# A decoder layer on one core: division order, statistics order, first feed-forward quarters and the output bias

## The chip, the core and the metric

The kernel runs on one NeuronCore of a Trainium2 chip. The profile names its engines PE (TensorE, matrix products and transposes), DVE (VectorE), ACT (ScalarE), POOL (GpSimd) and SP (SyncE, which issues most transfers). PE writes only to PSUM, from where DVE and ACT take results; POOL works in SBUF. The metric is the device time of one execution in microseconds (us), as the median of several runs.

## The reference

A pre-norm decoder layer on x of 8 batches x 256 rows x 1024 features, all in float32:

```python
x = x + attn(layernorm(x))            # 32 heads of 32, binary weights with scales
x = x + xattn(layernorm(x), ctx)      # 16 heads over a context of 256 rows, low-rank keys and values
x = x + ffn(layernorm(x))

# ffn, INTER = 2752, RANK = 256
P = x @ U1
H = P @ V1 + b1
act = silu(H[..., :INTER]) * H[..., INTER:]
out = (act @ U2) @ V2 + b2
```

In the attentions the scores of a head go through a softmax: subtract the row's maximum, take the exponential, divide by the row's sum. In the cross-attention the context is projected once to 64 features (`C_kv = K @ Wkv_d`), which serve as keys and, projected up, as values.

## The kernel before

The work is tiled by 128 rows. One batch of 256 rows is two tiles. There are three phases, one after the other: self-attention of batches 0 to 7, cross-attention of batches 0 to 7, and the feed-forward in four blocks of four tiles (512 rows).

**Steps.** Both attentions run as a chain of steps: eight per batch in self-attention, four in cross-attention, four heads each. `step` (L676) issues the scores of its heads, the row maxima on DVE (L686, `nm`), the transposes of the step before's probabilities (`turned`, L518, copied by ACT at L526), the exponentials on ACT (L705, `p`), and at its end the weighted sums of the step before. What a step before the last still owes (`early` and `late`, for example the rescaled cross-attention output `y` at L667, which POOL adds to x at L674) stands in between.

**Parts.** Between these a step runs *parts*: pieces of other work that keep PE busy, such as projections of the next batch. A plan written out by hand (`self_plan`, `cross_plan`) says which parts go into which step, and the order of instructions on each engine is exactly the order in which the program issues them. `run_part` (L192) takes one part off the queue. A part may have a preparation of its own (`ahead`) that is issued before its main work; up to two parts marked `soon` have theirs issued at the start of the step (L691).

**Divisions.** In self-attention the probabilities are divided by their sums: a reciprocal (L556), then four multiplications by DVE (L566), or POOL or ACT for some heads. `step` issues the divisions of a pair of heads just before a part, as soon as the exponentials of that pair have been issued (the inner function `then`).

**Context parts.** In self-attention step 5 of the last batch, the parts are four transposes of the first cross-attention context (`ctx_parts`, L783, PE L163), copied in turn by ACT and DVE (L789, `cT`), and the projection that reads them (`ckv_part`, L799). In the other batches' context parts the step is a cross-attention step.

**Statistics.** The means and variances for the layer norms are pieces of DVE work (L138, L140, `statistics`), kept in the list `idle`. `run_part` issues one ahead of a part when enough credit has built up, which the parts' estimated lengths add to. A reader that needs them earlier takes all that are left (`need`). After a tile's last piece POOL computes the inverse deviation (L121, L122). In cross-attention the finished x of a batch leaves to memory from POOL's queue (`x_leave`, L872) in step 2 of the next batch.

**First feed-forward quarters.** `head_parts` (L975) normalizes a half of a tile (DVE L155, `xn`, two buffers), transposes it on PE (L997) and copies it out, by ACT or DVE in turn (L998, `xT`). A block has eight of these, and then two factors (L1008). Those of block 0 are the parts of the last cross-attention batch, four in each of steps 0 and 1; those of the later blocks run beside the block before. Their PSUM tile comes from the pool `psA` with two banks. Most other parts call `bank` (L107), which goes round three banks, two of `psA` and one of `psB`.

**Feed-forward.** For each of 22 column tiles of 128 (the last of 64), `hidden` makes gate and up (PE L1034), ACT the sigmoid (L1046), DVE the products (L1047, L1049), and `down` sums them two iterations later (PE L1078). `tail` (L1093) multiplies by V2 (PE L1097), adds b2 on DVE into `y` (L1105), adds `y` to x on POOL (L1107) and stores a tile of 512 KB (L1108). The tails of a block run in iterations 2 to 5 of the next block; those of the last block end the kernel.

Of the kernel before, what the change touches and what calls it, by code (L numbers as in the profile page):

```python
# [10 lines left out]
F32 = mybir.dt.float32  # L11
# [7 lines left out]
P = 128  # L19
# [16 lines left out]
def decoder_layer(  # L36
# [24 lines left out]
    nc = tc.nc  # L61
    B, S, E = x.shape
    NT = B * S // P
    TB = S // P
# [42 lines left out]
    def bank(shape, name):  # L107
        turn[0] += 1
        if turn[0] % 3 == 1:
            return psB.tile(shape, F32, tag="psB", name=name)  # L110
        return psA.tile(shape, F32, tag="psA", name=name)
# [38 lines left out]
    mv3 = [stat.tile([P, TB, 2], F32, name=f"mv3_{b}") for b in range(B)]  # L150
    rs3 = [stat.tile([P, TB], F32, name=f"rs3_{b}") for b in range(B)]

    def normed_half(x_, mv, rs, h):
        xn = wk_.tile([P, 512], F32, tag="xn", name="xn", bufs=2)
        nc.vector.tensor_scalar(  # L155
            xn, x_[:, h * 512 : (h + 1) * 512], mv, rs, ALU.subtract, ALU.mult
        )
        return xn
# [13 lines left out]
    def settle():  # L172
        now = list(ripe)
        ripe[:] = later
        later.clear()
        for f in now:
            f()
# [1 line left out]


    class Part:
        def __init__(self, us, main, ahead=None, soon=False):
            self.us, self.main, self.todo, self.soon = us, main, ahead, soon

        def ahead(self):
            if self.todo is not None:
# [2 lines left out]

    queue = []  # L190

    def run_part(then=None):  # L192

        settle()
        if idle and credit[0] > 2.0:
            credit[0] -= 2.0
            idle.pop(0)()
        if then is not None:
            then()
        p = queue.pop(0)  # L200
        p.ahead()
        if queue:
            queue[0].ahead()
        p.main()
        credit[0] = min(credit[0] + p.us, 4.5) if idle else 0.0


    qT_w = [wt.tile([P, EC, P], F32R, tag=f"qw{c}", name=f"qT_w{c}") for c in range(EC)]
# [467 lines left out]
    def step(cur, prev, parts, extra=None):  # L676

        s = cur.scores()
        nm = small.tile([P, 4, TB], F32, tag="nm", name="nm")
        cur.sm = small.tile([P, TB, 4], F32, tag="sm", name="sm")  # L680
        due = prev.prev if prev is not None else None
        if due is not None:
            due.early()
        pTs = []
        for j in range(4):
            nc.vector.tensor_reduce(nm[:, j, :], s[j], AX.X, ALU.max, negate=True)  # L686
            if prev is not None:
                pTs.append(turned(prev.p[j]))
        for p in queue[: min(parts, 2)]:
            p.ahead()  # L690
        soon = [p for p in queue[:parts] if p.soon][:2]  # L691
        if isinstance(due, Cross):
            for p in soon:
                p.ahead()
        if due is not None:
            due.late()
        for p in soon:
            p.ahead()
        cur.p, cur.prev = [], prev
        exps = []  # L700

        def exp(j, t):
            if t == 0:
                cur.p.append(wk_.tile([P, TB, S], F32, tag="p", name="p", bufs=4))
            nc.scalar.activation(  # L705
                cur.p[j][:, t, :], s[j][:, t, :], AF.Exp,
                bias=nm[:, j, t : t + 1], accum_out=cur.sm[:, t, j : j + 1],
            )

        exps = [(j, t) for j in range(4) for t in range(TB)]  # L710


        divided = isinstance(cur, Self)
        pe, sc = 0.0, (0.5 if prev is not None else 3.0) if divided else 1.0
        pairs = [0, 1]
        for k in range(parts):
            pe += queue[0].us
            while exps and sc < pe:
                exp(*exps.pop(0))
                sc += 0.49  # L720

            if divided and not pairs and queue[0].us > 1.0:
                cur.over_sums_end()

            def then():
                while k and divided and pairs and len(exps) <= 4 - 4 * pairs[0]:
                    cur.over_sums(pairs.pop(0))

            run_part(then)
            if k == 0 and extra is not None:  # L730
                extra()
        for e in exps:
            exp(*e)
        for i in pairs:
            cur.over_sums(i)
        cur.over_sums_end()
        if not parts and extra is not None:
            extra()
        if prev is not None:
            prev.weighted(pTs)  # L740
            prev.prev = None
        return cur
# [40 lines left out]
    def ctx_parts(st, copies):  # L783
        def main(q):
            t, h = q // 2, q % 2
            if q == 0:
                st.cT = wk_.tile([P, EC, S], F32, tag="xh", name="cT")
            ps = four_T(st.c[t][:, h * 512 : (h + 1) * 512], "ps_c")
            copies[h](st.cT[:, h * 4 : (h + 1) * 4, t * P : (t + 1) * P], ps)  # L789

        return [Part(0.5, lambda q=q: main(q)) for q in range(2 * TB)]

    def ckv_part(st):
        def main():
# [180 lines left out]
    def head_parts(fb):  # L975


        def ahead(q):
            j, h = q // 2, q % 2
            b = fb.i * 2 + j // TB  # L980
            need(fb.half[j // TB])
            fb.xn = getattr(fb, "xn", {})
            fb.xn[q] = normed_half(
                fb.x[j], mv3[b][:, j % TB, 0:1], rs3[b][:, j % TB : j % TB + 1], h
            )

        def main(q):
            j, h = q // 2, q % 2
            if q == 0:
                fb.xT = [  # L990
                    wk_.tile([P, 4, W], F32, tag="qT", name="xT0", bufs=2),
                    wk_.tile([P, 4, W], F32, tag="xl", name="xT1"),
                ]
            ps = psA.tile([P, 4, P], F32, tag="psA", name="ps_t")
            xn = fb.xn.pop(q)
            for k in range(4):
                nc.tensor.transpose(ps[:, k, :], xn[:, k * P : (k + 1) * P], ident)  # L997
            (dve if h else act)(fb.xT[h][:, :, j * P : (j + 1) * P], ps)  # L998

        def factor(r):  # L1000
            if r == 0:
                if fb.i % 2 == 0:
                    fb.pT = wk_.tile([P, RC, W], F32, tag="xh", name="pT")
                else:
                    fb.pT = fw.late[:, 0:RC, :]
            ps = psA.tile([P, W], F32, tag="psA", name="ps_p")
            for e in range(EC):
                nc.tensor.matmul(  # L1008
                    ps,
                    fw.u1[:, e, r * P : (r + 1) * P],  # L1010
                    fb.xT[e // 4][:, e % 4, :],
                    start=(e == 0),
                    stop=(e == EC - 1),
                )
            (dve if r else act)(fb.pT[:, r, :], ps)

        return [Part(0.5, lambda q=q: main(q), lambda q=q: ahead(q), True) for q in range(2 * BT)] + [
            Part(7.0, lambda r=r: factor(r)) for r in range(RC)
        ]
# [73 lines left out]
    def tail(fb, j):  # L1093
        for h in range(E // 512):
            ps = psA.tile([P, 512], F32, tag="psA", name="ps_o")
            for r in range(RC):
                nc.tensor.matmul(  # L1097
                    ps,
                    fb.zT[:, r, j * P : (j + 1) * P],
                    fw.v2[:, r, h * 512 : (h + 1) * 512],  # L1100
                    start=(r == 0),
                    stop=(r == RC - 1),
                )
            y = wk_.tile([P, 512], F32, tag="y", name="y", bufs=2)
            nc.vector.tensor_add(y, ps, fw.b2[:, h * 512 : (h + 1) * 512])  # L1105
            xs = fb.x[j][:, h * 512 : (h + 1) * 512]
            nc.gpsimd.tensor_add(xs, xs, y)  # L1107
        nc.sync.dma_start(of[fb.i * BT + j], fb.x[j])  # L1108

# [128 lines left out]
    with tc.manual_schedule(  # L1240
# [84 lines left out]
        for n in range(2, len(pairs) + lag):  # L1325
            fb, f = pairs[n] if n < len(pairs) else (None, n)
            if fb is not None:
                hidden_next(n)
                if fb.i == 0 and f == 3:
                    x_leave(xts[B - 1])  # L1330
                elif idle:
                    idle.pop(0)()
                if fb.i + 1 < NB:
                    if f == 6:
                        ffn_x(fbs[fb.i + 1])
                    if f == 8:
                        hp = head_parts(fbs[fb.i + 1])
                        queue.extend(hp)
                        queue[0].ahead()
                    if 9 <= f < 9 + len(hp):  # L1340
                        run_part()
            m = n - lag
            down(*pairs[m], *acs.pop(m))
            if fb is not None and fb.i and 2 <= f < 2 + BT:
                tail(fbs[fb.i - 1], f - 2)
# [36 lines left out]
```

## Time and profile before

| what | value |
|---|---|
| time, median of 3 runs | 1556.1 us (1555.15 to 1556.22) |
| profiled execution | 1556.36 us |
| its span | 1554.6 us |
| mean granted clock of PE | 0.995 |
| PE busy from 0 to 100 us | 79.39 us |
| PE busy from 660 to 940 us | 277.47 us of 280 |
| PE busy from 940 to 960 us | 17.24 us of 20 |
| PE busy from 1134 to 1534 us | 400.00 us of 400 |
| last matmul ends, last POOL addition ends | 1548.9 us, 1551.0 us |

The profile is one execution of the program. Its span runs from the first to the last recorded instruction; the execution's own time is 1.76 us longer. A row of the time order gives start, length, engine, line, operation, output from input, and in brackets how long the engine stood idle before it and what released it. A row with "x4" merges four instructions. Starts of neighbouring DVE instructions lie closer than their lengths, since they overlap a little. PEld is PE's weight load, which overlaps its matmuls. A busy PE is not PE at its peak.

Self-attention runs to about 638 us, cross-attention to about 989, the feed-forward to the end.

### The profile page before, as it was taken

The numbers are of one execution on the slowest core, as the hardware profiler recorded it, in microseconds if no ns is written. First come the engines' busy times: TensorE is split into PE (matmuls) and PEld (weight loads), VectorE is DVE, ScalarE is ACT, GpSimd is POOL, SyncE is SP. The second block draws the span as 40 slices with busy tenths as digits, with TensorE's granted clock in tenths as the row PEclk, the third lists the DMA queues.
The fourth block names the chain that finished last, engine by engine and source line by source line (L and its number), as shares of the span: only waits on it lengthen the run. The fifth ranks groups of instructions, "written<-read, shape, count | busy, mean of one in ns | idle before, by whom it ended". The sixth has DMA issues, their size and how long they took to land.

```text
span 1554.6 us, 25703 instructions
## 1 busy us (share of the span) xinstructions
PE 1510.9 (97%) x9494; PEld 1014.8 (65%) x9494; DVE 964.1 (62%) x1880; ACT 799.8 (51%) x2448; POOL 404.7 (26%) x491
## 2 busy tenths in 40 slices
PE   6899999999999999999999999999999999999998
PEld 5777888788878786777778776544444444444443
DVE  7878999999989898766676665343233233423322
ACT  4677898989888888755565666311101111111110
POOL 2555443445354534022221111100020002001102
PEclk9989999999999999999999999999999999999999
DMA  8430020101020141211453311110001002000001
GB/s 233 67 82 26 18 69 28 55 29 67 17 69 29 60 150 44 86 42 61 154 187 132 113 61 77 48 54 0 0 41 68 1 0 108 0 1 27 28 0 54
DMA packets 65612, 92.78 MB, mean 60 GB/s; under 512 B 40218, under 2 KB 46160, under 8 KB 65360
## 3 DMA queue, kind: packets, MB, share of 16 engines
q1 hardware_dynamic: 60880, 74.37, 15.2%
q0 software_dynamic: 4608, 16.78, 2.7%
q8 instruction: 75, 1.23, 0.3%
q14 instruction: 49, 0.40, 0.1%
HBM read 65.44 MB, written 25.17 MB: 58 GB/s over the span
## 4 chain that ended last, share of the span: by engine, by line
PE 78%; DVE 10%; ACT 6%; DMA 2%; issue 1%; POOL 1%; SPq 1%; POOLq 0%; DVEq 0%; ACTq 0%
PE ps_h L1034 19%; PE ps_z L1078 9%; PE ps_pt L522 9%; PE ps_q L397 6%; PE ps_o L490 5%; ACT p L705 4%; PE s L619 4%; PE ps_p L1008 4%; PE po L642 4%; PE ps_o L1097 3%; PE s L543 3%; PE po L581 3%; DVE nm L686 2%; PE ps_o L659 2%; PE ps_q L848 2%; PE ps_qk L863 2%
## 5 line engine op out<-in xcount | busy, mean ns | idle before, releaser
L705 ACT ACTIVATE p<-s,nm 128x256 f32<-128x256 f32 x768 | 357.9, 517 | 0.4 <-DVE nm L686 0.4
L526 ACT COPY pT<-ps_pt 128x512 f32<-128x512 f32 x384 | 198.6, 598 | 178.1 <-PE ps_pt L522 177.3
L1046 ACT ACTIVATE sg<-ps_h,b_col 128x512 f32<-128x512 f32 (+1 forms) x88 | 59.7, 678 | 413.5 <-PE ps_h L1034 413.5
L686 DVE TENSOR_REDUCE nm<-s 128x2 f32<-128x512 f32 x384 | 237.3, 677 | 9.9 <-PE s L619 6.8
L1047 DVE SCALAR_TENSOR_TENSOR sg<-ps_h,b_col,sg 128x512 f32<-128x512 f32 (+1 forms) x88 | 64.9, 738 | 272.2 <-ACT sg L1046 272.2
L522 PE MATMUL ps_pt<-ident,p 128*128 128x128 f32 x1536 | 195.7, 278 | 4.8 <-DVE xl L343 3.2
L522 PEld LDWEIGHTS ps_pt<-ident,p 128*128 128x128 f32 x1536 | 164.4, 141 | 45.6 <-issue 25.5
L705 ACT ACTIVATION_READ_ACCUMULATOR p<-s,nm 128x1 f32 x768 | 190.9, 249 | 0.0
L1107 POOL TENSOR_TENSOR x2t<-x2t,y 128x512 f32<-128x512 f32 x32 | 40.6, 1267 | 480.3 <-DVE y L1105 480.3
L1078 PE MATMUL ps_z<-ac,u_sb 128*128 128x512 f32 x336 | 157.7, 593 | 0.0
L397 PE MATMUL ps_q<-xh,qT_w 128*128 128x256 f32 x496 | 121.8, 287 | 0.0
L397 PE MATMUL ps_q<-xl,qT_w 128*128 128x256 f32 x496 | 118.9, 281 | 0.0
L674 POOL TENSOR_TENSOR x1t<-x1t,y 128x256 f32<-128x256 f32 x64 | 47.5, 764 | 234.6 <-DVE y L667 234.6
L1078 PEld LDWEIGHTS ps_z<-ac,u_sb 128*128 128x128 f32 x336 | 61.9, 190 | 68.8 <-issue 68.8
L490 PE MATMUL ps_o<-oT_w,oh 128*128 128x512 f32 x256 | 105.9, 414 | 0.0
L350 POOL TENSOR_SCALAR tmp<-y 128x512 f32<-128x512 f32 x78 | 57.2, 733 | 183.7 <-DVE y L499 106.4
L490 PE MATMUL ps_o<-oT_w,ol 128*128 128x512 f32 x256 | 101.0, 395 | 0.0
L566 DVE TENSOR_SCALAR p<-p,sm 128x256 f32<-128x256 f32 x252 | 90.1, 414 | 8.0
L397 PEld LDWEIGHTS ps_q<-xh,qT_w 128*128 128x128 f32 x496 | 93.3, 188 | 1.6
L397 PEld LDWEIGHTS ps_q<-xl,qT_w 128*128 128x128 f32 x496 | 93.4, 188 | 0.0
L1034 PE MATMUL ps_h<-pT,w_ffn 128*128 128x512 f32 (+1 forms) x184 | 88.7, 577 | 0.0
L1034 PE MATMUL ps_h<-late,w_ffn 128*128 128x512 f32 (+1 forms) x184 | 88.7, 577 | 0.0
(159 smaller groups left out, 2737.0 us busy)
## 6 DMA issues: line engine op xcount, KB each, us to landing
xs<-in_x_dram SPq DMA_DIRECT2D x32, 512.0 KB, 4.1
x<-xs POOLq DMA_DIRECT2D x16, 512.0 KB, 3.0
x1t<-x SPq DMA_DIRECT2D x16, 512.0 KB, 5.2
c<-in_ctx_dram SPq DMA_DIRECT2D x16, 512.0 KB, 3.8
x<-x1t POOLq DMA_DIRECT2D x16, 512.0 KB, 3.8
x2t<-x SPq DMA_DIRECT2D x16, 512.0 KB, 5.8
out_dram<-x2t SPq DMA_DIRECT2D x16, 512.0 KB, 2.6
w<-in_L_attn_q_weight_dram SPq DMA_DIRECT2D x32, 128.0 KB, 5.9
```

The lines of the kernel that those rows point to most:

```text
L397: nc.tensor.matmul(ps[:, i, :], w(i, e), x_[:, e, :], start=(e == 0 and x_ is st.xh), stop=(e == EC - 1 and x_ is st.xl),)
L490: nc.tensor.matmul(ps, o_[c // 4][:, c % 4, t * P : (t + 1) * P], oT_w[:, c, h * 512 : (h + 1) * 512], start=(c == 0 and o_ is st.oh), sto ...
L522: nc.tensor.transpose(ps[:, k, t * P : (t + 1) * P], p[:, t, k * P : (k + 1) * P], ident)
L526: nc.scalar.copy(pT, ps)
L566: nc.vector.tensor_scalar_mul(p, p, self.sm[:, t, j : j + 1])
L619: nc.tensor.matmul(s[2 * i + j][:, t, :], st.cqk[p0 : p0 + XD, 2 * c + i, t * P : (t + 1) * P], st.ckv[p0 : p0 + XD, :], start=True, stop= ...
L642: nc.tensor.matmul(self.po[XD * j : XD * (j + 1), i, :], self.st.ckvT[:, k, :], pTs[2 * i + j][:, k, :], start=(k == 0), stop=(k == TB - 1),)
L686: nc.vector.tensor_reduce(nm[:, j, :], s[j], AX.X, ALU.max, negate=True)
L705: nc.scalar.activation(cur.p[j][:, t, :], s[j][:, t, :], AF.Exp, bias=nm[:, j, t : t + 1], accum_out=cur.sm[:, t, j : j + 1],)
L1034: nc.tensor.matmul(ps[h * n : h * n + n], v1_of(r, i, f, n), fb.pT[:, r, h * w_ : (h + 1) * w_], start=(r == 0), stop=(r == RC - 1),)
L1047: nc.vector.scalar_tensor_tensor(sg[:m], hs[0][:m], bg, sg[:m], ALU.add, ALU.mult)
L1078: nc.tensor.matmul(fb.zs[r], fw.u2[f // 4][:n, f % 4, r * P : (r + 1) * P], ac[:n], start=(k == 0), stop=(k == NF - 1 and COPIES < 2),)
```

## The change

There are four edits.

- **Divisions.** A part can be marked `hold`; the context parts are. While the next part is so marked, `step` does not issue divisions before it.
- **Statistics.** `run_part` can take a piece of statistics behind the part instead of ahead of it. Cross-attention steps do.
- **First quarters.** In the last batch up to four parts instead of two have their preparation issued at the start of the step. The third and fourth of each four use the buffers of tag `z`. Block 0's transposes take their PSUM from `bank`.
- **Bias.** POOL adds b2 to the block's x (a whole tile of 128 x 1024 at once), issued in iterations 10 to 13 of the block itself. `tail` adds the product to that x directly on DVE, `y` goes, and each half of a tile is stored by itself.

```diff
-    def normed_half(x_, mv, rs, h):
-        xn = wk_.tile([P, 512], F32, tag="xn", name="xn", bufs=2)
+    def normed_half(x_, mv, rs, h, tag="xn"):
+        xn = wk_.tile([P, 512], F32, tag=tag, name="xn", bufs=2)
...
-    def run_part(then=None):
-
-        settle()
+    def piece_due():
         if idle and credit[0] > 2.0:
             credit[0] -= 2.0
             idle.pop(0)()
+
+    def run_part(then=None, behind=False):
+
+        settle()
+        if not behind:
+            piece_due()
         if then is not None:
             then()
...
         p.main()
         credit[0] = min(credit[0] + p.us, 4.5) if idle else 0.0
+        if behind:
+            piece_due()
...
-        soon = [p for p in queue[:parts] if p.soon][:2]
+        soon = [p for p in queue[:parts] if p.soon][: 4 if cur.st.b == B - 1 else 2]
...
+            hold = queue[0].hold
...
-                while k and divided and pairs and len(exps) <= 4 - 4 * pairs[0]:
+                while k and divided and not hold and pairs and len(exps) <= 4 - 4 * pairs[0]:
                     cur.over_sums(pairs.pop(0))
 
-            run_part(then)
+            run_part(then, not divided)
...
-        return [Part(0.5, lambda q=q: main(q)) for q in range(2 * TB)]
+        return [Part(0.5, lambda q=q: main(q), hold=True) for q in range(2 * TB)]
...
-                fb.x[j], mv3[b][:, j % TB, 0:1], rs3[b][:, j % TB : j % TB + 1], h
+                fb.x[j], mv3[b][:, j % TB, 0:1], rs3[b][:, j % TB : j % TB + 1], h,
+                "z" if fb.i == 0 and q % 4 >= 2 else "xn",
             )
...
-            ps = psA.tile([P, 4, P], F32, tag="psA", name="ps_t")
+            if fb.i == 0:
+                ps = bank([P, 4, P], "ps_t")
+            else:
+                ps = psA.tile([P, 4, P], F32, tag="psA", name="ps_t")
...
-            y = wk_.tile([P, 512], F32, tag="y", name="y", bufs=2)
-            nc.vector.tensor_add(y, ps, fw.b2[:, h * 512 : (h + 1) * 512])
             xs = fb.x[j][:, h * 512 : (h + 1) * 512]
-            nc.gpsimd.tensor_add(xs, xs, y)
-        nc.sync.dma_start(of[fb.i * BT + j], fb.x[j])
+            nc.vector.tensor_add(xs, ps, xs)
+            nc.sync.dma_start(of[fb.i * BT + j][:, h * 512 : (h + 1) * 512], xs)
...
+                if 10 <= f < 10 + BT:
+
+                    xs = fb.x[f - 10]
+                    nc.gpsimd.tensor_add(xs, xs, fw.b2)
```

More of the change, by code (lines that the diff above doesn't have):

```diff
@@ L181, in decoder_layer, with __init__ @@
     class Part:
-        def __init__(self, us, main, ahead=None, soon=False):
-            self.us, self.main, self.todo, self.soon = us, main, ahead, soon
+        def __init__(self, us, main, ahead=None, soon=False, hold=False):
+            self.us, self.main, self.todo, self.soon, self.hold = us, main, ahead, soon, hold
         def ahead(self):
```

## The prediction

> **What bounds the kernel now.** I read the page's busy shares and its chain of waits first, then the list of what PE (TensorE) waited for, whole and cut into stretches, and last the order of time of PE, DVE and ACT around each edit.
>
> ```profile
> PE 1510.9 (97%) x9494; PEld 1014.8 (65%) x9494; DVE 964.1 (62%) x1880; ACT 799.8 (51%) x2448; POOL 404.7 (26%) x491
> PE 78%; DVE 10%; ACT 6%; DMA 2%; issue 1%; POOL 1%; SPq 1%; POOLq 0%; DVEq 0%; ACTq 0%
> ...
> PE ps_t L997 <- DVE xn L155: 2.4, 3, 0.9
> ...
> PE ps_k L799 <- DVE cT L789: 2.3, 2, 1.5
> ...
> PE ps_t L997 <- DVE y L667: 0.4, 1, 0.4
> ```
>
> PE is busy for all but 43.7 us, so an edit can gain only where PE stands still or behind PE's last matmul. The columns of a wait are total, times and longest. Most of the standstill lies in the first 100 us, untouched here. The edits can reach three places: 1.46 us at the context projection, 2.8 us at the feed-forward's first quarters (the two L997 rows), and the run-out at the end. Between 1010 us and 1534 us PE waits for nothing.
>
> **1. Divisions behind the context copies** (batch 7, self-attention step 5). DVE, then PE, in order of time (start, length):
>
> ```profile
> 615.84 0.68 DVE L789 COPY cT<-ps_c 128x512 f32<-128x512 f32 x1
> 617.36 0.18 DVE L556 RECIPROCAL sm<-sm 128x4 f32<-128x4 f32 x1 [0.84 <-ACT p L705]
> 617.57 1.24 DVE L566 TENSOR_SCALAR p<-p,sm 128x256 f32<-128x256 f32 x4
> 618.74 0.68 DVE L789 COPY cT<-ps_c 128x512 f32<-128x512 f32 x1
> ```
> ```profile
> 616.57 1.44 PE L799 MATMUL ps_k<-cT,w_down 128*64 128x128 f32 x18 [0.85 <-DVE cT L789]
> 619.47 1.09 PE L799 MATMUL ps_k<-cT,w_down 128*64 128x128 f32 x14 [1.46 <-DVE cT L789]
> ```
>
> The second copy has had its transposes since 615.7 (16 from 613.63, 2.09 us), yet stands behind a reciprocal that waits for ACT's exponentials, and four divisions. The instruction order of the changed kernel puts the two copies side by side and the reciprocal with its four divisions after them. The second copy then runs 616.45 to 617.1; PE needs it at 618.0. The wait of 1.46 goes whole. The 0.85 before it, for the first copy, stays. What is late next: the four divisions still end at 618.8, as before. The second pair waits for ACT's last exponential (619.15) and for the two projection copies, whose matmuls now end near 619.1; it is done by about 620.6 on DVE and 620.9 on ACT (two of 0.46). The transposes that read it begin at 622.56 - 1.46 = 621.1: covered by 0.2 us, and by 1 us for the later heads. **-1.46** (ends -1.2 and -1.5).
>
> **2. Moments behind parts in cross-attention.** By the two kernels' instruction orders only four statistics and one aggregate move there, each to the other side of one reciprocal; from then on the last pieces come one place earlier, in the feed-forward, where PE waits for nothing. The reciprocal is read two steps (20 us) later. PE has no wait for a statistic or that reciprocal in 640 to 940. Behind the moved rows in batch 3, the inverse deviation (0.22 and 0.72 us on POOL) goes ahead of two stores of x2 on POOL's queue. They were issued at 802.8; now they wait for the aggregate after the projection's copy (804.5 + 0.7 + 0.2) and start near 806.3, 3.5 us later. SP's loads of the next x1 tiles (806.6) wait for these stores (3.4 to land), so move to about 810, and the six v1b loads behind them too. They land by about 815; DVE reads x1 at 820.09. Without that cover each us late would cost a us. v1b is read after 989. **0** (-0.3 to +0.5).
>
> **3. First quarters by four** (batch 7, cross steps 0 and 1).
>
> ```profile
> 941.61 0.99 DVE L155 TENSOR_SCALAR xn<-x2t,mv,rs 128x512 f32<-128x512 f32 x2
> 943.11 0.69 DVE L667 TENSOR_TENSOR y<-ps_o,sm 128x512 f32<-128x512 f32 x1 [0.51 <-PE ps_o L659]
> 943.72 0.54 DVE L155 TENSOR_SCALAR xn<-x2t,mv,rs 128x512 f32<-128x512 f32 x1
> 944.17 0.68 DVE L998 COPY xT<-ps_t 128x512 f32<-128x512 f32 x1
> ```
> ```profile
> 942.84 1.04 PE L997 MATMUL ps_t<-ident,xn 128*128 128x128 f32 x8
> 944.40 0.63 PE L997 MATMUL ps_t<-ident,xn 128*128 128x128 f32 x4 [0.52 <-DVE xn L155]
> 945.96 0.63 PE L997 MATMUL ps_t<-ident,xn 128*128 128x128 f32 x4 [0.93 <-DVE xn L155]
> ```
>
> PE waits 0.52 + 0.93 here and 0.38 + 0.93 in step 1, together 2.76. Now four xn stand ahead of y: starts 0.46 apart, so 941.61, 942.07, 942.53, 942.98, and y runs 943.45 to 944.14 (was 943.11). The xn are never late again. What is late next is a PSUM bank: the transposes now take banks from the rotation of three, so the third quarter gets the bank of ps_o, which y frees. PE is ready at 943.9, starts at 944.2: a new wait of 0.3. The fourth takes the bank that ACT's first copy frees at 944.06, no wait. Quarters end at 945.25 instead of 946.51. In step 1 the softmax side gains less: the eight exponentials still end near 948.2 (ACT is busy throughout), so the row maxima start 949.0 instead of 949.56 and end 951.4; three xn and y then end at 953.4. PE, at its third quarter by 953.0, waits 0.45. Quarters end near 954.5 instead of 956.87. Behind y stand POOL's additions to x1 (0.35 later, read 20 us later) and one xT copy, needed before the factors, with 5 us of room. **-2.3**; ends -2.76 (no bank wait) and -1.4 (step 1's gain lost to the exponentials).
>
> **4. Bias added to x ahead.** The end, on DVE and POOL:
>
> ```profile
> 1549.01 0.69 DVE L1105 TENSOR_TENSOR y<-ps_o,b_sb 128x512 f32<-128x512 f32 x1 [1.02 <-PE ps_o L1097]
> 1549.78 1.26 POOL L1107 TENSOR_TENSOR x2t<-x2t,y 128x512 f32<-128x512 f32 x1 [0.46 <-DVE y L1105]
> ```
>
> DVE's addition keeps its shape (PSUM and SBUF to SBUF, 0.69), but stores follow it directly: ready at 1549.70 instead of 1551.04, -1.34. The last store is half of 512 KB. In the DMA view of the last 5 us the whole one moves data for 1.3 us, so -0.6 if the rate holds; the remaining 3.55 - 1.3 us behind it stay. **-1.94** (-1.3 to -2.2).
>
> Here a rule speaks against the edit. The Trainium skill ("DMA: Bandwidth & Descriptors", Bandwidth) says to batch transfers to 1 MiB or more; its fit (first part of the page) is about 2.0 us fixed plus bytes by 436 GB/s. By that, as an estimate, a half takes 2.6 us, and if halves went one after another, eight would need 20.8 us from 1537.7, ending at 1558.5 against 1553.2 for the data today: +5.3 instead of -1.94. The row decides: a store is issued every 1.72 us per half and its data take 0.65, the DMA engines stand idle between, and no instruction waits for a landing before the last.
>
> POOL's 32 additions of 1.27 become 16 of 128x1024, about 2.54 each (an estimate, twice the row), 40.6 us as before. They wait only for x2t and for the xn that read it, so POOL runs block 0's four as soon as its statistics are done (about 1030), and the others behind each pair of xn. Nothing but later ones is queued behind them. The second rule: the skill's "SBUF — State Buffer" (Who interferes with whom) has a DVE tensor_scalar in its two-port mode and a POOL instruction exclude one another for a whole instruction. The trace's xn agree in kind: 0.54 usually, up to 1.49 beside POOL. By the row an xn loses at most 0.95, by the rule 2.54. Both fit: xn ends at 1041.4, its transposes come at 1045.6, 4.2 us later. **0** by either. In the middle tails y's double buffer also goes; PE did not wait there.
>
> **Sum.** 1.46 + 0 + 2.3 + 1.94 = 5.7 us. The profiled execution took 1556.36 (span 1554.6 and 1.76 around it): 1550.7. It was 0.26 above the median of three, 1556.1; on that basis 1550.4. I say **1550.5**.
>
> **Rivals.**
> - *The step maxima and exponentials take the place of PE's wait.* Part 3 shrinks to -1.4 or less, part 1's cover of 0.2 us proves short and costs back 0.7: -0.7 - 1.4 - 1.3 = -3.4, 1552.7. For it: ACT has no idle in step 0 from 943.5. Against: the long factor step after it (7 us of matmuls) lets DVE and ACT catch up.
> - *Only the end shows.* The moved copies and quarters wait for something the trace doesn't name (instructions fetched, banks in another order after eight more turns of the rotation): -1.9, 1554.4, no change. Against: the waits name their releaser, and the new order removes it.
> - *Slower: a bank wait long enough to drop the clock.* Place: the third quarters, where PE now waits for y. Granted clock is 1.00 from 100 to 1534, but in the start-up, where PE stands still for loads, it falls (stretch, length, busy time of PE, PEld, DVE, ACT, POOL, then granted clock, DMA share, GB/s):
>
> ```profile
> 28.00:61.00 33.00, 27.25 (x233) 24.33 (x232) 27.23 (x54) 19.53 (x58) 14.30 (x32) 0.95 0.55 107
> 72.00:100.00 28.00, 23.13 (x188) 17.79 (x188) 21.01 (x39) 20.50 (x65) 11.39 (x19) 0.82 0.42 95
> ```
>
>  The second stretch lost 0.18 x 28 = 5.0 us. The skill ("TensorE: Matmul & The Clock Gate", Part 1) puts the drop at one idle window of about 3.4 us. So this decides from a stall of 3.4 us on: twice 3.4 + 5.0, less the 2.76 no longer waited, is +14; with parts 1 and 4, 1556.4 + 14 - 3.4 = 1567. Against: my two bank waits are 0.3 and 0.45.
>
> **How the numbers follow.** A difference counts here from 0.2%, 3.1 us (below 1553.0 or above 1559.2). The forecast has 0.64, the first rival 0.16 (nearly all still below 1553.0), only-the-end 0.14, slower 0.06, the last with what I don't see. Faster 0.79, same 0.15, slower 0.06. The ends of the parts add to -3.4 (1.2 + 1.4 + 1.3, less 0.5) and -6.8 (1.5 + 0.3 + 2.76 + 2.2), so 1552.7 and 1549.3 on the median; half of only-the-end is taken in: 1549.0 to 1553.8.
>
> **What would show it.** Step 1: the 1.46 before L799's second group gone, cT copies 0.6 apart. Step 3: no ps_t wait for xn; two waits of 0.3 to 0.5 for y. Step 4: the last DVE addition followed by a 256 KB store, no POOL work in the last 100 us, PE still without waits from 1010. Wrong if ps_k waits for something new, if x1's load shows up before xn near 820, or if feed-forward iterations lengthen while POOL adds the bias.

## The result, and the profile after

| | before | changed |
|---|---|---|
| median, 6 runs each | 1555.92 us | 1550.63 us (1550.0 to 1551.94) |
| profiled execution, its span | 1556.36, 1554.6 us | 1550.99, 1549.2 us |

The ratio is 0.9968, with a 95% interval of 0.9956 to 0.998: faster by 0.3%. The forecast was 1550.5.

The page's busy line of the changed kernel, and three rows of what PE waited for (total, times, longest):

```profile
PE 1509.7 (97%) x9494; PEld 1014.9 (66%) x9494; DVE 963.9 (62%) x1880; ACT 798.3 (52%) x2448; POOL 401.5 (26%) x475
...
PE ps_o L665 <- DVE ol L658: 1.7, 2, 1.5
...
PE ps_k L806 <- DVE cT L796: 0.9, 1, 0.9
...
PE ps_t L1008 <- DVE y L673: 0.5, 2, 0.3
```

Of two waits at the context projection one is left, and the 2.8 us at the first quarters have become 0.5. The row for `ol`, the copied cross-attention output, is as it was before. Busy shares tell nothing of it: no engine's busy time changed by more than 3.2 us.

To see where the 5.4 us of span went I cut both executions at the same PE instructions, by their starts in the order of time. All figures are differences of such starts, in us:

| stretch | before | changed | difference |
|---|---|---|---|
| start to the first context transpose | 613.63 | 613.95 | +0.32 |
| to the weighted sums behind the projection (edit 1) | 6.85 | 5.16 | -1.69 |
| to the first cross-attention scores | 17.31 | 17.30 | -0.01 |
| cross-attention, to the first quarter (edit 2) | 305.05 | 305.01 | -0.04 |
| the quarters, to the first factor (edit 3) | 20.70 | 18.69 | -2.01 |
| to the first feed-forward matmul | 25.35 | 25.44 | +0.09 |
| to the first down matmul | 15.05 | 15.04 | -0.01 |
| to the last tail | 530.96 | 530.96 | 0.00 |
| last tail to the end (edit 4) | 19.70 | 17.65 | -2.05 |

The start-up, which no edit touches, differs by 0.32. Over the profiles of this case it ran from 612.65 to 613.95, so the start-up alone can move a run by 1.3. The other stretches of an unchanged place repeat within 0.1 us, which lets single profiles measure tenths that medians cannot.

**The context projection after.** DVE, then PE, in order of time (start, length, what the engine did, in brackets the wait before it):

```profile
616.16 1.27 DVE L796 COPY cT<-ps_c 128x512 f32<-128x512 f32 x2
617.66 0.18 DVE L562 RECIPROCAL sm<-sm 128x4 f32<-128x4 f32 x1 [0.23 <-ACT p L711]
617.88 1.26 DVE L572 TENSOR_SCALAR p<-p,sm 128x256 f32<-128x256 f32 x4
```
```profile
616.89 2.29 PE L806 MATMUL ps_k<-cT,w_down 128*64 128x128 f32 x32 [0.85 <-DVE cT L796]
```

The copies stand side by side, and the 32 matmuls are one group. They last 2.29 us where the two groups before lasted 1.44 + 1.09: besides the wait of 1.46 the broken run had cost 0.24. One of these matmuls is 0.27 long, so 32 of them in 2.29 overlap; at a break the overlap is lost. That this is all of the 0.24 is argued, not tested.

**The quarters after**, PE:

```profile
941.42 1.04 PE L1008 MATMUL ps_t<-ident,xn 128*128 128x128 f32 x8
942.75 1.09 PE L1008 MATMUL ps_t<-ident,xn 128*128 128x128 f32 x8 [0.29 <-DVE y L673]
943.78 1.95 PE L648 MATMUL po<-pT,ckv 128*64 128x256 f32 x16
945.65 2.31 PE L625 MATMUL s<-ckv,cqk 64*128 64x256 f32 x16
...
951.99 1.09 PE L1008 MATMUL ps_t<-ident,xn 128*128 128x128 f32 x8 [0.19 <-DVE y L673]
953.01 1.95 PE L648 MATMUL po<-pT,ckv 128*64 128x256 f32 x16
954.89 2.42 PE L625 MATMUL s<-ckv,cqk 64*128 64x256 f32 x16
```

Besides the waits for y, look at the lengths: the scores of step 1 and step 2 take 2.31 and 2.42, where they took 2.00 before. In the kernel before, ACT's last exponential of step 0 had ended at 948.30, before PE began the scores of step 1 (ACT, then PE):

```profile
947.80 0.50 ACT L705 ACTIVATE p<-s,nm 128x256 f32<-128x256 f32 x1
```
```profile
948.39 2.00 PE L619 MATMUL s<-ckv,cqk 64*128 64x256 f32 x16
...
958.75 2.00 PE L619 MATMUL s<-ckv,cqk 64*128 64x256 f32 x16
```

Now no wait is printed, since the stop falls inside a merged row, but PE has come so early that the scores' banks still hold those of the step before. ACT reads the last of them to 946.69, 1.04 after PE's start at 945.65 (`n_copies_dve` below tests this):

```profile
946.18 0.51 ACT L711 ACTIVATE p<-s,nm 128x256 f32<-128x256 f32 x1
946.54 0.24 ACT L711 ACTIVATION_READ_ACCUMULATOR p<-s,nm 128x1 f32 x1
```

**The end, and POOL's new work.** The last DVE row, and the first rows of POOL's bias additions:

```profile
1545.59 0.69 DVE L1116 TENSOR_TENSOR x2t<-ps_o,x2t 128x512 f32<-128x512 f32 x1 [0.97 <-PE ps_o L1108]
```
```profile
1026.04 9.46 POOL L1345 TENSOR_TENSOR x2t<-x2t,b_sb 128x1024 f32<-128x1024 f32 x4
1038.12 2.35 POOL L1345 TENSOR_TENSOR x2t<-x2t,b_sb 128x1024 f32<-128x1024 f32 x1 [2.63 <-DVE xn L155]
```

Behind the last addition come the store of half a tile and the end, 1549.2 - 1546.28 = 2.9 us later (3.55 behind POOL's last row before). The 16 bias additions take 2.35 us each.

### The profile page after: what moved, and what is told of

The parts are those of the page before. It is cut to its first block, busy times and chain, and to the rows that moved or that the text cites. A ratio compares the mean times of both kernels' runs of the same rounds, so it can differ in the third digit from the quotient of the medians.

```text
span 1549.2 us, 25717 instructions
## 1 busy us (share of the span) xinstructions
PE 1509.7 (97%) x9494; PEld 1014.9 (66%) x9494; DVE 963.9 (62%) x1880; ACT 798.3 (52%) x2448; POOL 401.5 (26%) x475
## 4 chain that ended last, share of the span: by engine, by line
PE 80%; DVE 10%; ACT 6%; issue 1%; POOL 1%; DMA 1%; SPq 0%; DVEq 0%; ACTq 0%; POOLq 0%
PE ps_h L1045 19%; PE ps_z L1089 9%; PE ps_pt L528 9%; PE ps_q L403 7%; PE ps_o L496 5%; ACT p L711 4%; PE ps_p L1019 4%; PE ps_o L1108 4%; PE s L625 3%; PE po L648 3%; PE s L549 3%; PE po L587 3%; DVE nm L692 2%; PE ps_q L855 2%; PE ps_qk L870 2%; PE ps_v L470 2%
## 5 line engine op out<-in xcount | busy, mean ns | idle before, releaser
L1345 POOL TENSOR_TENSOR x2t<-x2t,b_sb 128x1024 f32<-128x1024 f32 x16 | 37.6, 2356 | 296.2 <-DVE xn L155 296.2
```

## The experiments

My theory was that each edit's gain sits at its own place and is neither shared nor given back. The first rival was that a later point would have held PE anyway, so that an edit taken away costs less than its row of the table.

**Each edit taken away.** `u_hold`:

```diff
-        return [Part(0.5, lambda q=q: main(q), hold=True) for q in range(2 * TB)]
+        return [Part(0.5, lambda q=q: main(q)) for q in range(2 * TB)]
```

> The changed kernel with the context parts no longer marked hold, so the divisions go back between the two context copies. Theory (each part's gain sits at its own place): PE's second wait at the context projection comes back, 1.4 to 1.7 us, and the whole kernel is slower than the changed one by that, about 1552.2. Rival (the gain is shared: a later point, such as the step's maxima, would have held PE anyway): under 0.7 us, about 1551.0.

`u_quarters` (`[:2]` in `step`, tag `xn`, `psA`, as before):

> The changed kernel with the first quarters as before: two prepared at the start of a step, two buffers, two banks. Theory: the four waits of 2.76 us in all come back and the 1.2 us that the changed kernel loses there (0.48 waiting for y, 0.7 in stretched scores) go: slower by 2.0, about 1552.6. Rival (the long factor step that follows would let PE catch up anyway): under 1 us.

`u_bias` (the tail as before, no addition ahead):

> The changed kernel with the tail as before: b2 added by DVE into y, y added by POOL, whole tiles stored. Theory: slower by 2.05 us, all of it behind the last matmul, about 1552.7; the feed-forward before it unchanged. Rival (POOL's long additions also cost or save DVE time beside the next block's quarters): the time from 1010 us to the last matmul differs by more than 0.3 us.

`u_moments`:

```diff
-            run_part(then, not divided)
+            run_part(then)
```

> The changed kernel with a statistics piece always ahead of its part. Theory: no difference, within 0.3 us, and PE's order in time in cross-attention the same to 0.1 us. Rival (the moved statistics do free DVE for something PE waits for, or hold it): 0.5 us or more either way between 640 and 940 us.

| kernel | median (runs) | over the changed 1550.63 | at its own place |
|---|---|---|---|
| u_hold | 1552.42 (7) | +1.79 | 6.85: +1.69 |
| u_quarters | 1552.57 (10) | +1.94 | 20.71: +2.02 |
| u_bias | 1552.41 (8) | +1.78 | 19.71: +2.06 |
| u_moments | 1550.67 (4) | +0.04 | 305.08: +0.07 |

The four were timed in another session than the changed kernel (the kernel before at 1556.23 there, at 1555.92 with the result). Against `u_moments` of their own session the first three lose 1.75, 1.90 and 1.74, so the comparison holds. In each, all other stretches but the start-up stay within 0.1 us of the changed kernel's. The wait that returned in `u_hold`:

```profile
618.54 1.09 PE L806 MATMUL ps_k<-cT,w_down 128*64 128x128 f32 x14 [1.49 <-DVE cT L796]
```

So three edits carry the gain, one does nothing measurable, and the rival falls.

**Which half of edit 3 works.** It has two parts: four preparations ahead, and a third PSUM bank. `q_two_banks` keeps the first alone, `q_ahead_two` the second alone.

> The changed kernel with four quarters prepared ahead, but their transposes in the two banks of psA as before. Theory of the prediction: the waits for xn are gone by the four preparations, and the third quarter now waits for ACT's first copy (942.64 by the changed kernel's times) instead of y (942.70), the fourth for DVE's copy behind y: the stretch from the first quarter's transposes to the first factor is within 0.2 us of the changed kernel's 18.69. Rival (the third bank carries the gain): longer by 0.6 or more.

> The changed kernel with the rotation of three banks, but two quarters prepared ahead as before. Theory: the waits for xn come back, the stretch from the first quarter to the first factor is that of the kernel before, 20.70 (changed kernel 18.69). Rival (the third bank carries the gain): under 19.5.

`q_ahead_two` took 20.70, as expected: without early xn the third bank brings nothing. `q_two_banks` took 19.28, a miss for me: 0.59 longer than the changed kernel, most of it in step 1:

```profile
950.98 1.09 PE L1005 MATMUL ps_t<-ident,xn 128*128 128x128 f32 x8 [0.58 <-DVE y L673]
952.43 0.66 PE L1005 MATMUL ps_t<-ident,xn 128*128 128x128 f32 x4 [0.35 <-DVE xT L1006]
```

In step 0 no quarter waited for y; there the third waited 0.24 for ACT's copy. In step 1 the second quarter waits for y, as it did in the kernel before (0.38): so `ps_o`, which y reads, stands there in one of the two banks. The fourth waits for DVE's copy of the second. y itself came no later against PE: it ended 1.17 us behind the start of the first quarter, and 1.27 in step 0. The early xn bring 1.4 of the 2.0, and the third bank 0.6 on top of them.

**Whole stores.** `d_whole_store` moves the store out of the loop over halves:

```diff
-            nc.sync.dma_start(of[fb.i * BT + j][:, h * 512 : (h + 1) * 512], xs)
+        nc.sync.dma_start(of[fb.i * BT + j], fb.x[j])
```

> The changed kernel with the bias added ahead, but each tile stored whole behind its second half. Theory: only the data of the last store count, 512 KB instead of 256 KB, so the time behind the start of the last tail is 0.6 us longer (18.25 instead of 17.65) and the kernel 0.6 slower. Rival (small stores pay their fixed part one after another, so whole ones are better): shorter, by up to 5 us.

The tail took 18.29 against 17.65. The median of 6 runs was 1551.3, 0.7 over the changed kernel; but in its session the kernel before took 1556.37, 0.45 more than with the result, so it is the tail that shows the 0.64. Data rate in 40 slices of one stretch near the end, first whole (6 us, slices of 0.15), then halves (5 us, slices of 0.125):

```profile
GB/s 410 410 164 0 0 0 0 0 0 0 0 0 0 0 0 0 109 355 382 437 437 410 410 437 410 110 0 0 0 0 0 0 0 0 0 0 0 0 0 0
```
```profile
GB/s 393 230 0 0 0 0 0 0 0 0 229 393 360 426 360 312 17 0 0 0 0 0 0 115 442 328 442 344 361 66 0 0 0 0 0 0 0 0 0 0
```

The last burst is about nine slices of 0.15, 1.3 us, whole and six of 0.125, 0.7 us, half, at about 400 GB/s both. The small stores keep the rate and lie well apart. The rule on batching (the Trainium skill, "DMA: Bandwidth & Descriptors", Bandwidth) did not bind here. The page measured it, and the fit that the prediction took, on transfers issued by GpSimd; these are stores issued by SP.

**The slower rival, forced.** The prediction gave a stall over 3.4 us as the point where the clock would fall. `p_stall` makes a stall longer than that:

```diff
+            if isinstance(cur, Cross) and cur.st.b == B - 1 and cur.c == 0:
+                for i in range(8):
+                    spare = small.tile([P, TB], F32, tag="rs1", name="spare")
+                    nc.vector.tensor_reduce(spare, s[i % 4], AX.X, ALU.max, negate=True)
             due.late()
```

> The changed kernel with eight more row maxima on DVE (0.6 us each, results unused) ahead of y in the first of the two steps, so that PE's third quarter waits about 5 us instead of 0.3. Nothing else is computed differently. Theory A (a stall costs its length): the stretch from the first quarter to the first factor grows by 4.5 to 5.0, to about 23.4, and the granted clock from 935 to 975 stays 1.00. Theory B (the slower rival of the prediction: a standstill of over 3.4 us drops the clock): a granted clock under 1.00 behind the stall and a stretch of 25 or more.

The stretch took 25.90, 7.21 over the changed kernel, and the time of its one run was 1558.13, beside 1556.37 for the kernel before. The stall itself was 5.07 instead of 0.29. Rows of 1 us each, of which the third figure from the end is the granted clock:

```profile
945.00:946.00 1.00, 0.00 (x0) 0.00 (x0) 1.00 (x2) 0.92 (x4) 0.00 (x0) 1.00 0.00 0
946.00:947.00 1.00, 0.00 (x0) 0.00 (x0) 1.00 (x3) 0.10 (x2) 0.00 (x0) 0.72 0.00 0
...
949.00:950.00 1.00, 1.00 (x6) 0.48 (x6) 0.56 (x1) 1.00 (x6) 0.06 (x1) 0.50 0.00 0
...
952.00:953.00 1.00, 1.00 (x8) 0.24 (x4) 0.15 (x1) 0.00 (x0) 0.00 (x0) 0.50 0.00 0
953.00:954.00 1.00, 1.00 (x10) 0.93 (x10) 0.69 (x1) 0.00 (x0) 0.00 (x0) 0.86 0.00 0
```

PE behind the stall:

```profile
947.43 1.97 PE L1012 MATMUL ps_t<-ident,xn 128*128 128x128 f32 x8 [5.07 <-DVE y L673]
949.33 3.68 PE L648 MATMUL po<-pT,ckv 128*64 128x256 f32 x16
```

PE stood still from about 942.4. The clock fell to half near 946.4, 4 us into the stall, and came back near 953.3, 6.8 us later. Theory B holds: 7.21 - 4.78 = 2.4 us came on top of the stall's own length. They are PE's own: the two groups behind the stall took 1.97 and 3.68, where they took 1.09 and 1.95 in the changed kernel, 2.6 more, and the scores and the wait of step 1 gave 0.2 back. The price of 5.0 per stretch that the prediction took from the start-up was twice too high. The limit of 3.4 us was too high as well. In the start-up of all 14 profiles the clock fell in a stall of PE of 3.01 to 3.05 us or within 1.3 us behind it; in the changed kernel near 37.5, with PE standing still from 34.75 to 37.80:

```profile
37.80 1.53 PE L338 MATMUL ps_d<-dg,ones 128*128 128x128 f32 x4 [3.05 <-POOL dg L331]
```
```profile
37.00:38.00 1.00, 0.20 (x1) 0.20 (x2) 0.86 (x4) 0.00 (x0) 1.00 (x3) 0.73 0.66 97
38.00:44.00 6.00, 6.00 (x32) 5.40 (x36) 2.75 (x9) 0.00 (x0) 1.45 (x5) 0.50 0.73 114
```

The longest stall past 100 us in that kernel, 1.53, left it at 1.00. What lies between was not tested. The change's waits of 0.29 and 0.19 are far below either.

**What is left at the quarters, and past them.** The changed kernel lost 0.48 there to y and 0.73 to stretched scores. Two edits aim at one each, a third at PE's longest wait behind it, which the change left alone:

```diff
# n_y_third
-            for p in soon:
+            for p in soon[:3]:
# n_copies_dve
-            (dve if h else act)(fb.xT[h][:, :, j * P : (j + 1) * P], ps)
+            (dve if h or fb.i == 0 else act)(fb.xT[h][:, :, j * P : (j + 1) * P], ps)
# n_early_first
         prev.weighted(pTs)
+        prev.early()
         hidden_next(1)
-        prev.early()
         prev.late()
```

> The changed kernel with y issued on DVE behind the third xn instead of the fourth. Theory (the changed kernel's scores in the steps behind the quarters end when ACT's exponentials let them, not when PE is free): both waits for y (0.29 and 0.19) go, but the stretched scores (2.31 and 2.42 us instead of 2.00) stretch by as much more; from the first quarter to the first factor 18.6 to 18.7, no gain. Rival (the bank wait is what the changed kernel lost against the forecast of 2.3): 18.2.

> The changed kernel with all copies of block 0's quarters on DVE, none on ACT. Theory: the eight exponentials of each step end about 1.1 us earlier, the scores take 2.0 us again in both, and the stretch from the first quarter to the first factor falls by 0.5 to 0.75, to 18.0. Rival (DVE, with four copies of 0.68 in each step, becomes late for the reciprocal and the row maxima): 18.7 or more.

> The changed kernel with the last cross-attention output copied out of PSUM (ol) before the second pair of feed-forward products instead of behind it. Theory: PE's wait of 1.53 us for ol, which no edit of the change touched, goes whole: from the first feed-forward matmul to the first down matmul 13.5 instead of 15.04, nothing given back later. Rival (the products then come late for the first down matmuls): 14.5 or more.

> The three together. Theory: the stretch of the quarters 17.5 to 17.6 (once the exponentials are early, the waits for y count too: 0.4 more than with the copies alone), the later one 13.5; in all 2.7 us under the changed kernel, about 1548.0, and 8 under the kernel before. Rival (the two waits take each other's place): 1.5 us or less.

| kernel | quarters (changed: 18.69) | to the first down matmul (15.04) | time (runs) |
|---|---|---|---|
| n_y_third | 18.70 | 15.05 | 1549.97 (1) |
| n_copies_dve | 18.07 | 15.05 | 1550.14 (1) |
| n_early_first | 18.70 | 13.27 | 1548.4 (1) |
| n_all | 18.67 | 13.27 | 1548.62 (5) |

`n_y_third` gains nothing: the waits for y are gone, and the scores are longer by as much (here of step 1):

```profile
944.38 2.55 PE L625 MATMUL s<-ckv,cqk 64*128 64x256 f32 x16
```

With the copies off ACT the scores are back at 2.00 and 0.62 is gained:

```profile
945.51 2.00 PE L625 MATMUL s<-ckv,cqk 64*128 64x256 f32 x16
```

Together the two gain 0.02 instead of the 1.1 that I expected. The fourth quarter takes the bank of the first one's copy, which on DVE now stands behind y and the fourth xn:

```profile
942.27 0.66 PE L1008 MATMUL ps_t<-ident,xn 128*128 128x128 f32 x4 [0.40 <-DVE xT L1009]
```

The early copy of the last output works: PE's wait for it is gone in `n_all`, and only the short one is left. It brought 1.77 where the wait was 1.53, again 0.24 more than the wait.

```profile
PE ps_o L665 <- DVE ol L658: 0.2, 1, 0.2
```

`n_all` is 1548.62 (1548.41 to 1549.33) beside 1555.78 for the kernel before, a ratio of 0.9953 (0.9939 to 0.9966), and of the 2.0 us that it has over the changed kernel 1.77 lie in that stretch and come from the third edit; 0.02 lie at the quarters, and the rest is no more than sessions and start-ups differ by. The same goes for the times of the single runs in the table: the stretches count there. By the table, `n_copies_dve` with `n_early_first` would be 0.6 better again; it was not run.

## Why the prediction was right, step by step

- **Edit 1**, forecast -1.46, measured -1.69. The mechanism was as put. The term left out was the 0.24 of the broken run of matmuls. That an edit can gain only where PE stands still was therefore not quite so: these 0.24 counted as busy. (And 20.6 of the 43.7 us of standstill lie in the first 100 us: the largest share, but not most.)
- **Edit 2**, forecast 0, measured -0.04, and +0.07 when taken away. The stores of x2 and the loads of x1 behind them did move about as worked out, by 3.6 and 2.9 us (stores 802.79 before, 805.03 after, loads 806.57 and 808.11, where everything else there came 1.4 earlier), and their cover held.
- **Edit 3**, forecast -2.3, measured -2.01. The four xn and the bank wait for y behaved as put, with 0.29 and 0.19 where I had 0.3 and 0.45. Up to the end of step 1's quarters the forecast was met: 953.01 - 941.42 = 11.59 us from the first quarter, where 954.5 - 942.84 = 11.66 had been worked out and 956.87 - 942.84 = 14.03 was before: 2.44 gained. The step that failed: I used the end of the exponentials to place the row maxima, but not to place the scores, which need the same banks. Step 1's scores became 0.31 longer; most of that counted nothing, since PE then waited 0.26 less for y than forecast. Step 2's scores, behind the last quarter, became 0.42 longer, and that is the shortfall: 2.44 - 0.42 = 2.02. `n_y_third` shows that these, not y, are the bound: an earlier y brings nothing. The low end of -1.4 had been laid to the same exponentials.
- **Edit 4**, forecast -1.94, measured -2.05. Both terms held: the store follows DVE (1.41 for 1.34 forecast), and half the bytes took half the time (0.64 for 0.6). From the first down matmul to the last tail nothing changed, so POOL's long additions beside DVE cost PE nothing. In the profile one xn beside them took 0.94, against 0.54 alone; a loss of 2.54, which the rule (the Trainium skill, "SBUF — State Buffer", Who interferes with whom) would allow, was not seen. This doesn't speak against the rule: that xn began at 1032.36, 0.65 before the end of the addition beside it, and ended after it, so there was little left to wait for.

```profile
1030.66 2.35 POOL L1345 TENSOR_TENSOR x2t<-x2t,b_sb 128x1024 f32<-128x1024 f32 x1
```
```profile
1032.36 0.94 DVE L155 TENSOR_SCALAR xn<-x2t,mv,rs 128x512 f32<-128x512 f32 x1
```

- **The sum.** The four edits and the 0.09 given back between them make 5.7 us, the forecast's own figure, as the extra in edits 1 and 4 covers the shortfall in edit 3. That the sum comes out to the tenth is luck; the three parts were off by 0.23, 0.29 and 0.11. The start-up took 0.3 of it back in the profiled run.
- **The rivals.** Neither sharing nor only-the-end occurred. The slower one needs a stall of the order of 3 us, which the change does not make.

## What to carry to other kernels

Where one engine is busy nearly throughout, list its few waits and ask of each edit which of them it removes and which buffer or bank is late next, also behind the stretch that it shortens; each gain here could then be measured at its own place, even where medians blur it. An earlier engine runs into the next release of a shared bank: count every user of the bank, and test fixes together, since two that aim at neighbouring waits can undo one another. Cutting the last store pays for half its data as long as the stores before it have drained.

## What the runs showed that I had not expected

A single stall of 5.07 us in the middle of a PE-bound kernel halved the granted clock for about 6.8 us and lengthened its stretch by 7.2 us; in the start-up it was halved already at a stall of 3.05. A group of matmuls broken by a wait lasts longer than the wait alone explains (2.53 against 2.29 us for 32). And POOL's 128x1024 addition took 2.35 us, less than twice the 1.27 of 128x512.
